# Two-layer pre-norm attention on one core: one more of the eight additions and the residuals given to adding DMA transfers, bias on ScalarE, v stored by channel halves

## The chip, the core and the metric

One core of a Trainium2 chip runs the whole program. The time is device microseconds of one execution, the median of the runs; a profiled execution of the same kernel gives the trace. Engines are named as in the profile: PE is TensorE (PEld its weight loads), DVE VectorE, ACT ScalarE, POOL GpSimd and SP SyncE. POOL and SP issue the DMA transfers; transfers that add into their destination are issued by POOL.

## The reference, cut to what matters

16 images of 256 channels x 32 x 32 go through two layers. Each layer normalises over groups of the last axis, projects q, k and v, and attends over the 1024 positions in 4 heads of 64 channels; the scores have a term of relative positions.

```python
xf = gn(x).reshape(b, 256, 1024)                   # 16 groups, eps 1e-5
q, k, v = (einsum('oc,bcn->bon', W, xf) + bias for W, bias in ...)
sim  = einsum('bhdi,bhdj->bhij', q, k)
qpos = einsum('hdi,bhdj->bhij', rel_h + rel_w, q)
attn = softmax(sim + qpos, axis=-1)
x = x + einsum('bhdn,bhmn->bhdm', v, attn).reshape(x.shape)   # twice, with the second layer's weights
```

Everything is float32. The bias of v can be added after the attention, since each row of `attn` sums to one.

## The kernel before

**Units, stages, blocks.** A unit is one image in one layer; 32 units run in a fixed order in which the second layer of an image comes at least four units after its first. A unit u has four blocks of work, one for each pair of heads `pr` (128 channels: channel half 0 or 1) and each half of 512 query positions. The text calls them b0 (pr 0, half 0), b1 (pr 0, half 1), b2 (pr 1, half 0) and b3 (pr 1, half 1). b0 is written out in `block_with_q` (every unit but the first), b3 in `block_with_values` (every unit but the last), b1 and b2 in `block`; the last unit's b2 and b3 are in `block_without_pieces`. T0 is the moment when TensorE ends b3, T1 when it ends b0, T2 b1 and T3 b2, so b3 runs from T3 to the next T0.

**One block.** For each of eight tiles j of 128 key positions: VectorE writes the term of positions into a PSUM tile (`seed`, L446), TensorE adds the scores (`scores`, L482), ScalarE takes the exponential into a tile p (L491). `add_up` (L521, L523) sums the tiles p on VectorE into `acc`; the last of them, j = 7, is added by a DMA transfer (`add_last`, L554). Then `fold`, `stack_up`, `fold_again` and `fold_stack` bring the partition sums down by further adding transfers (the rows of `stack` halve five times: D, R, R/2, R/4, R/8 with R = 32), `spread_sums` spreads them into `den_all` by four transfers of SP, and `reciprocals` (L633) takes them up on VectorE three to four blocks after the exponentials. TensorE meanwhile forms the products with v (`attend`, L537) in two stretches, and ScalarE copies the result out of PSUM into a tile `od` (`take_out`, L598). About a unit later `normalise` (L648) multiplies that tile by the reciprocals, and `add_residual` (L655) adds it and the bias of v to x, both on VectorE; a layer-1 unit's x is then stored by SP.

**Order.** Nothing is scheduled by a planner: each engine runs its instructions in the order in which the functions below issue them, and so do the queues of POOL and SP, whose transfers wait in line for what the first of them waits for. A transfer that adds to bytes that an earlier transfer writes waits, on POOL, until that one has landed. At the head of VectorE's work in b0, b1 and b2 stand the additions 5 and 6 of the block before; in b3 it is addition 6 alone, since 5 of b2 is made in b2.

**Between blocks.** In b3 the v of the next unit is formed by a scheme of seven products instead of eight (`Values`): its operands are sums of quarters of the normalised x, made by `sum_copies` on SP and `sum_additions` (L335) on POOL during b2. The group statistics of unit u+2 end in b3: rstd (L237) and nshift (L239) are computed on POOL, behind b3's transfers, and ScalarE applies them from b0 on (L248).

**Tiles in rings.** A tile's buffer is taken again when as many tiles of its tag have been allocated as there are buffers, and the first instruction that writes the new tile waits for the last that used the old one. `od` has three, p ten, `acc` three, x five:

```python
outs[u, pr] = opool.tile([P, 2, HALF], F32, tag="od", name=f"od_{u}_{pr}", bufs=3)   # L597, in take_out, half 0
before = blocks[n - 6][:2] if n > 5 else None       # b2: the tile (u-1, 0) is finished in this block
before = blocks[n - 5][:2] if n > 4 else None       # b3: the tile (u-1, 1)
```

In b2, `finish(*before)` comes ahead of that block's `take_out`, in b3 `normalise` and `add_residual` do. The PSUM bank from which b2's `take_out` reads is the one into which b3's first products of v go (`pw`, by the order in `ring`).

Of the kernel before, what the change touches and what calls it, by code (L numbers as in the profile page):

```python
# [9 lines left out]
F32 = mybir.dt.float32  # L10
# [3 lines left out]
ALU = mybir.AluOpType  # L14
# [3 lines left out]
P = 128  # L18
# [25 lines left out]
def flat(ap):  # L44
    return ap.rearrange("p w h -> p (w h)")
# [7 lines left out]
def fast_path(ctx, tc, sh, x, layers, out, W, den_all, good, flag):  # L53
# [26 lines left out]
    nc = tc.nc  # L80
# [119 lines left out]
    def filled(tag, name, value):  # L200
        pm = psum2(tag, name)[:, :, :G]
        nc.vector.memset(pm, value)
        return pm
# [82 lines left out]
    def values(u, g, pv):  # L286
        l = units[u][1]
        if g == 0:
            vts[u] = vpool.tile([P, NT, C], F32, tag="v", name=f"v_{u}")
        pv = pv.rearrange("p a (b c) -> p a b c", c=C)  # L290

        def products(t):
            for i in range(2):
                for cc in range(CC):
                    for rs, a in BANKS[t]:
                        for x, c in enumerate(QUARTERS):
                            j0 = (4 * g + 2 * a + i) * P + x * D
                            yield nc.tensor.matmul(
                                pv[c, a, i, :],
                                xns[u][rs, cc, j0 : j0 + D],  # L300
                                W.wv[l][rs, cc, :],
                                start=(t == 0 and cc == 0 and i == 0),
                                stop=(t == 1 and cc == CC - 1 and i == 1),
                                skip_group_check=True,
                            )

        def out_of_psum():
            nc.scalar.copy(
                vts[u][:, 4 * g : 4 * g + 4, :].rearrange("p (a b) c -> p a b c", a=2), pv
            )  # L310

        return stretches(products), out_of_psum
# [27 lines left out]
    class Values:  # L340

        def __init__(self, u, pw):
            l = units[u][1]
            x, t = quarters_of_x(u), sums_x[u]
            a11, a12, a21, a22 = W.blocks_of_v(l)
            d, s2, s3, s4 = (W.mixed[l][:, i, :] for i in range(4))
            self.pw = pw
            self.terms = {
                1: (0, x[:, 0, :], a11, True),
                2: (1, x[:, 2, :], a12, True),  # L350
                3: (0, x[:, 3, :], s4, False),
                4: (1, t[:, 3, :], a22, False),
                5: (0, t[:, 0, :], d, False),
                6: (0, t[:, 2, :], s2, False),
                7: (1, t[:, 1, :], s3, True),
            }
            vts[u] = vpool.tile([P, NT, C], F32, tag="v", name=f"v_{u}")
            self.v = vts[u]
            self.done = {}

# [35 lines left out]
            )  # L396

        def out(self, oc, nh):
            return self.v[:, nh * 4 : nh * 4 + 4, oc * P : (oc + 1) * P]

        def keep(self, oc, nh, sign):

# [38 lines left out]
    def seed(blk, j, tag):  # L441

        u, pr, half = blk
        ps = psum2(tag, f"ps_{u}_{pr}_{half}_{j}")
        ab = abt[u, pr][:, :, j, :]
        nc.vector.tensor_tensor(  # L446
            ps.rearrange("p h (w y) -> p h w y", y=H),
            ab[:, :, :H].unsqueeze(2).to_broadcast([P, 2, XH, H]),
            ab[:, :, H + half * XH : H + (half + 1) * XH]
            .unsqueeze(3)  # L450
            .to_broadcast([P, 2, XH, H]),
            ALU.add,
        )
        seeds[blk, j] = ps
# [60 lines left out]
    def add_up(blk, j):  # L515
        u, pr, half = blk
        if j == 0:
            return
        if j == 1:
            accs[blk] = apool.tile([P, 2, HALF], F32, tag="acc", name=f"acc_{u}_{pr}_{half}")  # L520
            nc.vector.tensor_tensor(accs[blk], probs[blk, 0], probs[blk, 1], ALU.add)  # L521
        else:
            nc.vector.tensor_tensor(accs[blk], accs[blk], probs[blk, j], ALU.add)  # L523
# [3 lines left out]
    def attend(blk, po):  # L527

        u, pr, half = blk

        def products(t, js=range(NT)):
            for j in js:
                p = probs[blk, j]
                for rs, a in BANKS[t]:
                    for h, c in enumerate(QUARTERS):
                        c0 = pr * P + h * D
                        yield nc.tensor.matmul(  # L537
                            po[c, a, :QUART],
                            vts[u][rs, j, c0 : c0 + D],
                            p[rs, h, a * QUART : (a + 1) * QUART],  # L540
                            start=(t == 0 and j == 0),
                            stop=(t == 1 and j == NT - 1),
                            skip_group_check=True,
                        )

        return stretches(products)
# [3 lines left out]
    R = P // 4  # L550
    stacks = {}

    def add_last(blk):
        nc.gpsimd.dma_start(accs[blk], probs[blk, NT - 1], accum_op=ALU.add)  # L554

    def fold(blk):

# [98 lines left out]
        if l == NL - 1:  # L656
            nc.sync.dma_start(flat(out[b, pr * P : (pr + 1) * P]), xs)

    def add_by_dma(u, pr):
        b, l = units[u]  # L660
        xs = xt[b][:, pr, :]
        nc.scalar.activation(xs, xs, AF.Identity, bias=W.bv[l][:, pr : pr + 1])
        nc.gpsimd.dma_start(xs, outs.pop((u, pr)).rearrange("p a n -> p (a n)"), accum_op=ALU.add)

    def store(u, pr):
        b = units[u][0]
        nc.sync.dma_start(flat(out[b, pr * P : (pr + 1) * P]), xt[b][:, pr, :])

    def finish(u, pr):
        normalise(u, pr)  # L670
        add_residual(u, pr)
# [85 lines left out]
    def block(n):  # L757
# [112 lines left out]
            add_up(blk, 5)  # L870
        if n in (2, 6):
            W.mix(n // 4)
        if before:
            finish(*before)
        if two and half == 1 or n == 0:
            mean_out()
        if stacked:
# [14 lines left out]
    def block_with_q(n):  # L892

        blk = blocks[n]
        u = blk[0]
        r0, r1, r2, r3 = ring
        previous, after, summed = blocks[n - 1], blocks[n + 1], blocks[n - 4][:2]
        folded = n - 1 < FOLDED
        add_up(previous, 5)
        add_up(previous, 6)  # L900
        add_last(previous)
        for j in range(1, 4):
            scores(blk, j)
        first, first_out = project(u, 1, "q", psum2(r3, f"pq_{u}_1"))
        first(0)
        norms(u, 0, 0)
        seed(blk, 4, r1)
        scores(blk, 4)
        norms(u, 0, 1)
        seed(blk, 5, r2)  # L910
        scores(blk, 5)
        add_up(blk, 1)
        fold_stack(*summed, R // 8)
        spread_sums(*summed)
        fold(previous)
        first(1)
        first_out()
        seed(blk, 6, r0)
        scores(blk, 6)
        stack_up(previous)  # L920
        add_up(blk, 2)
        seed(blk, 7, r1)
        scores(blk, 7)
        add_up(blk, 3)
        seed(after, 0, r2)
        add_up(blk, 4)
        if n in check:
            next(checks)
        norms(u, 0, 2)
        po = psum2(r3, f"po_{n}")  # L930
        values_of_p = attend(blk, po)
        values_of_p(0)
        scores(after, 0)
        fold_again(previous)
        ring[:] = r2, r0, r1, r3
        for j in range(1, 4):
            seed(after, j, ring[j % 3])
        reciprocals(*summed)
        norms(u, 0, 3)
        values_of_p(1)  # L940
        take_out(blk, po)
        pos[n] = po

    def block_with_values(n):
# [6 lines left out]
        two = u + 2 < NU  # L951
        v = Values(u + 1, psum2(r3, f"pw_{u + 1}"))

        add_up(previous, 6)
        scores(blk, 1)
        add_up(blk, 1)
        one = v.half(1, HI, False), v.half(1, LO, True)
        two_halves = score_half(blk, 2, 0), score_half(blk, 2, 1)
        v.stage("1", (two_halves[0], two_halves[1]), (one[0], one[1]), 0)
        add_last(previous)  # L960
        scores(blk, 3)
        v.stage("1", (two_halves[0], two_halves[1]), (one[0], one[1]), 1)
        v.keep(0, 0, 1.0)
# [20 lines left out]
        v.keep(1, 1, -1.0)  # L984
        fold_stack(*stacked, R)
        stack_up(previous)
        add_up(blk, 2)
        seed(after, 0, r1)
        v.combine(1, 1, ALU.subtract)
# [2 lines left out]
            next(checks)  # L992
        po = psum2(r2, f"po_{n}")
        values_of_p = attend(blk, po)
        values_of_p(0, range(NT // 2))
        v.pair("4", 3, 4, 0)
        if two:
            mean_out = norm_var(u + 2, filled(r0, f"pm_{n}", EPS / 2))
        values_of_p(0, range(NT // 2, NT))
        scores(after, 0)  # L1000
        v.pair("4", 3, 4, 1)
        v.keep(0, 1, -1.0)
# [12 lines left out]
        fold_stack(*stacked, R // 4)  # L1015
        seed(after, 2, r3)
        if before:
            add_residual(*before)
        seed(after, 3, r1)
        values_of_p(1)  # L1020
        take_out(blk, po)
# [9 lines left out]
    def block_without_pieces(n, half):  # L1031
# [39 lines left out]
        if not last:  # L1071
            after = blocks[n + 1]
            seed(after, 0, f0)
            add_up(blk, 4)
            values_of_p(0)
            scores(after, 0)
            seed(after, 1, f1)
            seed(after, 2, f2)
            reciprocals(*summed)
            normalise(*before)  # L1080
            add_by_dma(*before)
            seed(after, 3, f0)
            values_of_p(1)
            nc.gpsimd.drain()
            take_out(blk, po)
            return
# [450 lines left out]
```

## Time and profile before

| | us |
|---|---|
| median of 3 runs | 2628.89 |
| lowest and highest | 2628.64, 2631.62 |
| the profiled execution | 2630.66 |
| its span, first to last instruction | 2627.2 |
| PE busy | 2542.0 |
| DVE busy | 2340.3 |
| ACT busy | 1953.9 |
| POOL busy | 907.2 |

The span is what the trace covers; the profiled execution's own time is 3.5 us longer, for what lies around it. A busy PE is not a PE at its peak, since matmuls are pipelined and four small ones run beside one another on quarters of the array. Rows of a group give busy us, mean ns of one, and the idle time before with what ended it. A timeline row gives the start, the length and, in brackets, the idle time before. Two DVE instructions of 1.22 us in a row start 1.135 us apart. Of the DMA queues, q0 carries POOL's transfers, q1 SP's.

### The profile page before, as it was taken

What the parts mean: (1) busy time and instruction counts of PE and PEld (TensorE: products, weight loads), DVE (VectorE), ACT (ScalarE), POOL (GpSimd) and SP (SyncE); (2) the same over time, 40 slices, a digit from 0 to 9 for tenths busy, and PEclk for the clock granted to TensorE, in tenths of its full rate; (3) what the DMA queues carried; (4) which work ended last, traced back from release to release, by engine and by line L of the source; (5) the groups of instructions that cost most, each with busy time, mean ns of one, the idle gap of its engine ahead of it and who ended that gap; (6) DMA issues with size and microseconds to landing.
All of it is one profiled execution on the core that took longest, in us unless ns stands there. A gap on an engine that the chain in (4) does not pass through costs nothing.

```text
span 2627.2 us, 94070 instructions
## 1 busy us (share of the span) xinstructions
PE 2542.0 (97%) x41192; PEld 1419.2 (54%) x41192; DVE 2340.3 (89%) x2244; ACT 1953.9 (74%) x3917; POOL 907.2 (35%) x969
## 2 busy tenths in 40 slices
PE   8999999999999999999999999999999999999998
PEld 4555555555555555555555555555555555555554
DVE  7898998889888898998989888888889898898988
ACT  6778777778777787777877778777778777787654
POOL 1333333333333333333333333333333333333330
PEclk9999999999999999999999999999999999999999
DMA  3555545565556555556645565556565555555552
GB/s 92 110 112 114 107 97 107 118 138 116 99 117 136 113 114 103 111 117 126 124 102 112 113 128 114 114 112 116 120 138 115 106 97 117 112 108 101 104 117 75
DMA packets 158064, 295.23 MB, mean 112 GB/s; under 512 B 56392, under 2 KB 57928, under 8 KB 157648
## 3 DMA queue, kind: packets, MB, share of 16 engines
q0 software_dynamic: 75040, 170.74, 39.3%
q1 hardware_dynamic: 82608, 118.41, 15.0%
q8 instruction: 326, 5.34, 0.8%
q14 instruction: 90, 0.74, 0.1%
HBM read 51.78 MB, written 17.30 MB: 26 GB/s over the span
## 4 chain that ended last, share of the span: by engine, by line
PE 75%; DVE 18%; issue 3%; ACT 2%; DMA 1%; SPq 0%; DVEq 0%
PE po L537 27%; PE ps L482 26%; DVE ps L446 9%; PE pk L268 8%; PE pw L367 5%; PE pq L268 4%; DVE acc L523 4%; PE pa L423 2%; DVE acc L521 2%; DVE x L655 1%; DVE v L409 1%; ACT v L403 1%; PE ps L502 1%; ACT p L491 1%; DMA out_dram<-x 1%
## 5 line engine op out<-in xcount | busy, mean ns | idle before, releaser
L491 ACT ACTIVATE p<-ps,shift 128x1024 f32<-128x1024 f32 x993 | 1070.6, 1113 | 473.9 <-PE ps L482 462.2
L446 DVE TENSOR_TENSOR ps<-abt 128x1024 f32<-128x1024 f32 x1018 | 1229.3, 1228 | 144.6 <-ACT p L491 71.9
L482 PE MATMUL ps<-q,k 64*64 64x512 f32 x7944 | 994.8, 593 | 56.0 <-DVE ps L446 51.0
L537 PE MATMUL po<-p,v 64*64 64x256 f32 x16384 | 943.2, 376 | 1.2 <-issue 1.2
L537 PEld LDWEIGHTS po<-p,v 64*64 64x64 f32 x16384 | 653.3, 133 | 302.5 <-issue 61.3
L523 DVE TENSOR_TENSOR acc<-acc,p 128x1024 f32<-128x1024 f32 x643 | 780.7, 1214 | 6.0
L482 PEld LDWEIGHTS ps<-q,k 64*64 64x64 f32 x7944 | 293.4, 133 | 462.6 <-DVE ps L446 227.1
L583 POOL DMA_DIRECT2D stack<-stack x310 | 314.6, 1015 | 236.7 <-DMA stack<-stack 186.7
L578 POOL DMA_DIRECT2D stack<-acc x248 | 213.8, 974 | 345.5 <-DMA stack<-acc 289.9
L559 POOL DMA_DIRECT2D acc<-acc x124 | 104.4, 842 | 447.2 <-DMA acc<-p 439.7
L268 PE MATMUL pk<-xn,Wk 64*64 64x512 f32 x2048 | 242.9, 589 | 0.0
L268 PE MATMUL pq<-xn,Wq 64*64 64x512 f32 x2048 | 242.8, 589 | 0.0
L554 POOL DMA_DIRECT2D acc<-p x124 | 109.5, 883 | 359.9 <-ACT p L491 210.1
L248 ACT ACTIVATE xn<-x,nshift,rstd 128x128 f32<-128x128 f32 x496 | 209.5, 493 | 0.0
L190 ACT ACTIVATE junk<-x,neg 128x128 f32<-128x128 f32 x505 | 197.9, 400 | 0.0
L335 POOL DMA_DIRECT2D t<-xn x93 | 106.3, 1143 | 236.5 <-DMA t<-t 187.7
L598 ACT COPY od<-po 128x512 f32<-128x512 f32 x127 | 74.4, 586 | 137.7 <-PE po L537 137.7
L521 DVE TENSOR_TENSOR acc<-p,p 128x1024 f32<-128x1024 f32 x128 | 156.1, 1219 | 1.4 <-ACT p L491 1.4
L268 PEld LDWEIGHTS pq<-xn,Wq 64*64 64x64 f32 x2048 | 78.3, 133 | 140.9 <-issue 132.2
L268 PEld LDWEIGHTS pk<-xn,Wk 64*64 64x64 f32 x2048 | 75.2, 133 | 123.3 <-issue 123.0
L367 PE MATMUL pw<-mixed,t 64*64 64x128 f32 x2976 | 138.2, 273 | 3.5 <-issue 3.5
L367 PEld LDWEIGHTS pw<-mixed,t 64*64 64x64 f32 x2976 | 116.2, 133 | 45.4 <-DVE v L409 22.7
(95 smaller groups left out, 1915.8 us busy)
## 6 DMA issues: line engine op xcount, KB each, us to landing
acc<-p POOLq DMA_DIRECT2D x124, 512.0 KB, 5.1
rden<-rd SPq DMA_DIRECT2D x126, 256.0 KB, 5.2
acc<-acc POOLq DMA_DIRECT2D x124, 256.0 KB, 3.9
t<-xn POOLq DMA_DIRECT2D x62, 512.0 KB, 5.8
x<-in_x_dram SPq DMA_DIRECT2D x32, 512.0 KB, 4.2
stack<-acc SPq DMA_DIRECT2D x248, 64.0 KB, 2.2
stack<-acc POOLq DMA_DIRECT2D x248, 64.0 KB, 3.1
t<-xn SPq DMA_DIRECT2D x31, 512.0 KB, 3.4
```

The source lines that it names most:

```text
L190: nc.scalar.activation(junk, grouped(xt[units[u][0]], g), func, accum_out=into[:, g : g + 1], **bias)
L248: nc.scalar.activation(grouped(xns[u], g), grouped(xt[units[u][0]], g), AF.Identity, bias=shift[:, g : g + 1], scale=rstd[:, g : g + 1],)
L268: yield nc.tensor.matmul(pk[c, nh, :], w[l][rs, cc, c0 : c0 + D], xns[u][rs, cc, nh * HALF : (nh + 1) * HALF], start=(t == 0 and cc == 0), ...
L367: yield nc.tensor.matmul(self.pw[c, a, part * P : (part + 1) * P], x[rs, j0 : j0 + D], w[rs, :], start=first and not whole and part == 0, ...
L446: nc.vector.tensor_tensor(ps.rearrange("p h (w y) -> p h w y", y=H), ab[:, :, :H].unsqueeze(2).to_broadcast([P, 2, XH, H]), ab[:, :, H + h ...
L482: nc.tensor.matmul(ps[c, h, :], a[hs, j0 : j0 + D], b[hs, columns], start=bool(tag) and i == 0, stop=i == len(terms) - 1, skip_group_check ...
L491: nc.scalar.activation(p, ps, AF.Exp, bias=W.shift)
L521: nc.vector.tensor_tensor(accs[blk], probs[blk, 0], probs[blk, 1], ALU.add)
L523: nc.vector.tensor_tensor(accs[blk], accs[blk], probs[blk, j], ALU.add)
L537: yield nc.tensor.matmul(po[c, a, :QUART], vts[u][rs, j, c0 : c0 + D], p[rs, h, a * QUART : (a + 1) * QUART], start=(t == 0 and j == 0), s ...
L578: nc.gpsimd.dma_start(at, acc[R:D, h, :], accum_op=ALU.add)
L583: nc.gpsimd.dma_start(stack[:rows_], stack[rows_ : 2 * rows_], accum_op=ALU.add)
```

## The change

- `add_last` gets a first tile: in b0 and b3 it adds tiles 6 and 7 of the block before by two transfers, one after the other into the same `acc`, and `add_up(previous, 6)` goes from VectorE. In b3 it moves from behind the first products of v to the head of the block.
- `add_residual` is replaced for units 0 to 29: `normalise` stays, and `add_by_dma` adds the `od` tile to x by a transfer of POOL (512 KB), in b2 for half 0 (behind the last `sum_additions`) and in b3 for half 1 (at its end). The bias is added to x ahead of that, by ScalarE in b3 (`bias_x`, two instructions), a unit before the transfer.
- The stores of layer-1 units move with it: half 0's from b2 to b3 (behind `stack_up`), half 1's from b3 to b0 (ahead of the reciprocals' store).
- v is laid out as [channel half][tile][128] instead of [tile][256], so that a half's four tiles are one run of 512 elements where `keep` and `combine` write; `attend` reads its weights from there.
- In b3 five tiles' products with v, not four, stand ahead of the fourth pair of v's products, and three, not four, behind it.

```diff
-            vts[u] = vpool.tile([P, NT, C], F32, tag="v", name=f"v_{u}")
+            vts[u] = vpool.tile([P, CC, NT, P], F32, tag="v", name=f"v_{u}")
...
         def out(self, oc, nh):
-            return self.v[:, nh * 4 : nh * 4 + 4, oc * P : (oc + 1) * P]
+            return self.v[:, oc, nh * 4 : nh * 4 + 4, :]
...
-                            vts[u][rs, j, c0 : c0 + D],
+                            vts[u][rs, pr, j, h * D : (h + 1) * D],
...
-    def add_last(blk):
-        nc.gpsimd.dma_start(accs[blk], probs[blk, NT - 1], accum_op=ALU.add)
+    def add_last(blk, j0=NT - 1):
+        for j in range(j0, NT):
+            nc.gpsimd.dma_start(accs[blk], probs[blk, j], accum_op=ALU.add)
...
-    def add_by_dma(u, pr):
+    def bias_x(u, pr):
         b, l = units[u]
         xs = xt[b][:, pr, :]
         nc.scalar.activation(xs, xs, AF.Identity, bias=W.bv[l][:, pr : pr + 1])
+
+    def add_by_dma(u, pr):
+        xs = xt[units[u][0]][:, pr, :]
         nc.gpsimd.dma_start(xs, outs.pop((u, pr)).rearrange("p a n -> p (a n)"), accum_op=ALU.add)

     def store(u, pr):
-        b = units[u][0]
-        nc.sync.dma_start(flat(out[b, pr * P : (pr + 1) * P]), xt[b][:, pr, :])
+        b, l = units[u]
+        if l == NL - 1:
+            nc.sync.dma_start(flat(out[b, pr * P : (pr + 1) * P]), xt[b][:, pr, :])
...
# block (b2)
-        if before:
+        if before and last_unit:
             finish(*before)
+        elif before:
+            normalise(*before)
+            add_by_dma(*before)
...
# block_with_q (b0)
+        before = blocks[n - 6][:2] if n > 5 else None
         add_up(previous, 5)
-        add_up(previous, 6)
-        add_last(previous)
+        add_last(previous, NT - 2)
...
+        if before:
+            store(*before)
         reciprocals(*summed)
...
# block_with_values (b3)
-        add_up(previous, 6)
+        add_last(previous, NT - 2)
         scores(blk, 1)
...
-        add_last(previous)
         scores(blk, 3)
...
         stack_up(previous)
+        if before:
+            store(before[0], 0)
...
-        values_of_p(0, range(NT // 2))
+        values_of_p(0, range(5))
         v.pair("4", 3, 4, 0)
         if two:
+            for pr in range(CC):
+                bias_x(u, pr)
             mean_out = norm_var(u + 2, filled(r0, f"pm_{n}", EPS / 2))
-        values_of_p(0, range(NT // 2, NT))
+        values_of_p(0, range(5, NT))
...
         if before:
-            add_residual(*before)
+            add_by_dma(*before)
```

More of the change, by code (lines that the diff above doesn't have):

```diff
@@ L308, in out_of_psum @@
             nc.scalar.copy(
-                vts[u][:, 4 * g : 4 * g + 4, :].rearrange("p (a b) c -> p a b c", a=2), pv
+                vts[u][:, :, 4 * g : 4 * g + 4, :].rearrange("p o n c -> p n o c"),
+                pv.rearrange("p a b (o c) -> p (a b) o c", c=P),
             )
@@ L356, in __init__ @@
             }
-            vts[u] = vpool.tile([P, NT, C], F32, tag="v", name=f"v_{u}")
+            vts[u] = vpool.tile([P, CC, NT, P], F32, tag="v", name=f"v_{u}")
             self.v = vts[u]
@@ L535, in products @@
                     for h, c in enumerate(QUARTERS):
-                        c0 = pr * P + h * D
                         yield nc.tensor.matmul(
                             po[c, a, :QUART],
-                            vts[u][rs, j, c0 : c0 + D],
+                            vts[u][rs, pr, j, h * D : (h + 1) * D],
                             p[rs, h, a * QUART : (a + 1) * QUART],
@@ L1080, in block_without_pieces @@
             normalise(*before)
+            bias_x(*before)
             add_by_dma(*before)
```

## The prediction

> **What bounds the kernel now.** I read the busy row, then the stages of one unit, the chain of waits of b0, and the queues on both sides of T3.
>
> ```profile
> PE 2542.0 (97%) x41192; PEld 1419.2 (54%) x41192; DVE 2340.3 (89%) x2244; ACT 1953.9 (74%) x3917; POOL 907.2 (35%) x969
> ...
> core 0: us, PE busy (x) PEld busy (x) DVE busy (x) ACT busy (x) POOL busy (x), PEclk, DMA share, GB/s
> 1302.70:1325.14 22.44, 21.95 (x517) 16.64 (x512) 19.15 (x21) 12.15 (x14) 7.79 (x9) 1.00 0.57 119
> 1325.14:1344.90 19.76, 18.11 (x228) 8.23 (x224) 18.73 (x18) 15.65 (x33) 7.90 (x8) 1.00 0.33 57
> 1344.90:1363.16 18.26, 18.26 (x300) 9.60 (x296) 16.18 (x17) 16.34 (x36) 6.68 (x8) 1.00 0.52 102
> 1363.16:1383.80 20.64, 20.64 (x260) 9.79 (x256) 18.42 (x17) 17.41 (x43) 6.77 (x7) 1.00 0.75 159
> ```
>
> These are b3, b0, b1, b2: 81.1 us per unit. TensorE fills b1 and b2 to the end; a lighter VectorE is worth nothing there. In b0 it has 1.65 us without work, and 2.55 in all against back-to-back products (scores 0.86 us a tile, projections 1.72, value products 3.45, from the timeline's steps: 8 x 0.86 + 2 x 1.72 + 2 x 3.45 = 17.2). The chain of b0 names the cause:
>
> ```profile
> 1324.46 1.19 DVE x L655
> 1325.64 1.14 DVE ps L446
> 1326.79 1.14 DVE acc L523
> ...
> 1329.09 2.36 DVE ps L446 x2
> ```
>
> The residual (L655) and additions 5 and 6 stand before the seed for which TensorE waits. The change removes two of these three. So its aim is right; its price is on two in-order queues:
>
> ```profile
> 1377.78 1.22 POOL L335 DMA_DIRECT2D t<-xn  x1 [6.40 <-DMA t<-t]
> 1384.04 0.86 POOL L335 DMA_DIRECT2D t<-xn  x1 [2.62 <-DMA t<-xn]
> 1386.51 0.85 POOL L554 DMA_DIRECT2D acc<-p  x1 [1.61 <-DMA stack<-acc]
> 1393.56 0.81 POOL L559 DMA_DIRECT2D acc<-acc  x1 [5.33 <-DMA acc<-p]
> 1403.12 3.23 POOL L237 TENSOR_TENSOR rstd<-var,mhalf 128x16 f32<-128x16 f32 x1
> 1406.43 1.32 POOL L239 TENSOR_TENSOR nshift<-neg,rstd 128x16 f32<-128x16 f32 x1
> ...
> 1383.86 0.59 ACT L598 COPY od<-po 128x512 f32<-128x512 f32 x1 [0.39 <-PE po L537]
> 1401.76 1.11 ACT L491 ACTIVATE p<-ps,shift 128x1024 f32<-128x1024 f32 x1 [5.20 <-PE ps L482]
> ...
> acc<-p POOLq DMA_DIRECT2D x124, 512.0 KB, 5.1
> x<-od POOLq DMA_DIRECT2D x1, 512.0 KB, 6.1
> ```
>
> POOL stands still until a transfer that its next one builds on has landed (1393.56); behind it wait rstd and nshift, which ScalarE needs at T0 + 3.9.
>
> **The change, part by part.**
>
> VectorE: 62 additions go (an addition every 1.135 us in the timeline) and 60 of the 62 residuals (1.19). In b0 seed 4 could then start when exponential 1 ends, T0 + 2.0 instead of T0 + 3.95, and the stage falls from 19.8 to about 17.5 (the 17.2 above plus 0.3 at seed 7). b3 is 22.4 in the mean, 22.1 in its quiet instances; with less on VectorE and the fifth product step (which covers some of the 0.95 us per unit for which weight loads wait on L409) I take 21.6. b2 gains nothing. Gain: 3.1 us per unit.
>
> v by halves: the same counts and sizes. L409 takes 688 ns for 512 elements and L446 1228 for 1024, so 1.05 ns per element beyond 148 ns fixed; the split rows show no toll to win back: 0 (±0.05 each).
>
> ScalarE: 60 biases at 1.14 (L662). Both go into the 5.20 us idle before 1401.76, where ScalarE waits for scores: 0, and up to 2.3 per unit if that cover is gone.
>
> SP: the two stores move behind stack_up. By the times below their data has landed before SP is there; each costs the reciprocals' store behind it 0.34 us of issue, which the 7 us from reciprocal to spread value hide: 0.
>
> POOL, 122 more transfers, about 0.55 us apart when they need not wait: two new waits.
>
> First, the `od` ring. It has three buffers; tile (u-1,0) is number 2u-2 and (u,1) is 2u+1: the same buffer. b2 of unit u ends with take_out writing (u,1). Before, the residual's read of (u-1,0) ended 2.5 us ahead of it. Now a 512 KB transfer reads that buffer, issued behind the last sum_addition, which goes out at T3 - 0.8 to T3 + 1.9 over the units (mean 0.2). So: issue at T3 + 1.0. Ahead of it the 256 KB of t has 1.6 us to move (q0 moved 170.74 MB in 39.3% of 16 engines' span, 3.17 us per 512 KB). Data to T3 + 6.0, landing at about T3 + 6.8; the measured 6.1 alone would give T3 + 7.1. take_out stands at T3 + 0.06 today and runs from 6.9: behind it all exponentials of b3, and TensorE's first value product, which takes the PSUM bank that it frees. b3: 21.6 + 6.9 = 28.5. Bounds 5.5 and 8.
>
> Does the stall halve the clock? The tail shows it:
>
> ```profile
> 2617.00:2620.00 3.00, 0.00 (x0) 0.00 (x0) 1.59 (x3) 0.59 (x1) 0.00 (x0) 1.00 0.03 1
> 2620.00:2623.00 3.00, 0.19 (x2) 0.11 (x2) 0.82 (x5) 0.00 (x0) 0.00 (x0) 0.77 0.22 87
> 2623.00:2627.00 4.00, 0.00 (x0) 0.00 (x0) 0.00 (x0) 0.00 (x0) 0.00 (x0) 0.50 0.06 14
> ```
>
> 0.77 over 2620 to 2623 puts the drop to half at 2621.6, 4.6 us after the last product. The Trainium skill (TensorE: Matmul & The Clock Gate, Part 1) says half speed after an idle window of about 3.4 us and full speed after as long a busy one; nothing in mid-run here shows it. By it each stall costs another 1.7 to 3.4 us of half-speed work; without it 0. I take 2.
>
> TensorE's sum: 28.5 + 2 + 17.5 + 18.3 + 20.6 = 86.9.
>
> Second, POOL's chain. Transfer 6 of b2 goes out at T3 + 1.6, behind t and x: data to 9.1, some more for the 512 KB of rden beside it (1.7 if all in its way), landing near 10.5. Only then can transfer 7 go (11.0), and fold follows at 16.1, where it was at 9.8: +6.3. Everything after it on POOL moves along: nshift ends at 30.3 (24.0 in this unit; over the units 1.2 earlier, so 29.1). T0 is now at 28.5 or later, so ScalarE just escapes. In b0 again: R/4, x of half 1 (+0.9), transfer 6 (+1.8) landing +8.9 (0.9 short of two times 3.17 in its queue), transfer 7, fold_stack R/8 +9.5; den_all 4.55 later than transfer 7 goes (as from 1410.65 now) at +13.4, four issues 3.3, landing 1.9 after the last: +18.7, so T3 + 47.8. VectorE wants it at T1 - 1.1 = 44.9 (46.9 with the slow clock). Behind the waiting reciprocal stand additions 5 and 6 and seed 4 of b1 (3.7 us), for which TensorE waits, then 14.5 of b1 (14.2 from that tile's products to T2 now, and 0.3 at seed 7) and 20.6 of b2: 47.8 + 3.7 + 14.5 + 20.6 = 86.6.
>
> A page prices this otherwise: the Trainium skill (DMA: Bandwidth & Descriptors, Anatomy of one DMA) has 2.0 us + bytes / 436 GB/s, so 3.2 for 512 KB. x would land at T3 + 4.2, the stall be 4.2, POOL's chain never last: 21.6 + 4.2 + 17.5 + 18.3 + 20.6 = 82.2, some 2664 us. The trace has 5.1 and 6.1 for these adding transfers; I use the trace.
>
> What else is held longer: p tiles 6 and 7 of b3 are read until T3 + 43 and overwritten (ten buffers) by b1's first exponentials, the later at T1 + 0.9, 46.9 or after: free, with 4 us to spare; if that cover is gone, ScalarE waits at the head of b1 as long as the transfer is late.
>
> Sum: 87.0 a unit, +5.9, in 30 units: +177. The profiled execution took 2630.7 (span 2627.2), 1.8 above the median of 2628.9; so 2808, or 2806 on the median.
>
> **The rivals.** A change under 0.2% (5 us) can't be told from none here.
> 1. *Both waits* (0.62): 2806; with contention 90 us a unit, 2900.
> 2. *Only the ring's wait, POOL's chain covered* (0.30, with or without clock): transfer 6 lands 5 us after issue, as acc<-p does at the median, and nshift moves by 3. Unit 84.9 without the slow clock: +3.8 x 30, 2743. With a stall of 5.5: 83.5, 2700. For it: 55% DMA share before, some 70% after. Against: acc<-p took 7.1 us at 1386.51 with less beside it.
> 3. *Faster: x lands before take_out wants the buffer* (0.06). One mechanism: POOL gets past sum_additions so early, or moves so fast, that the ring's wait is below the 3.1 us won. It decides at a landing at T3 + 3.1; fully hidden, 3.1 x 30: 2536. For it: the transfer's sources are ready at 1380.0. Against: it is queued behind 1384.04.
> 4. *Nothing moves* (0.02): the wait equals the gain, 2629.
>
> That the products or v's layout alone do the work is excluded by the 0 above.
>
> **How the numbers follow.** Forecast 2806, rival 1. The range runs from rival 2's lower end (2700, with a little for less wait: 2690) to rival 1's upper (2900); outside remain 3, 4 and some of the tails. Faster 0.06, same 0.02, slower 0.92.
>
> **What would show it.** L598 on ACT waits for DMA x<-od, 30 times, about 6.5 us each; a PE gap of 6 to 7 us at each start of b3, granted clock below 1.00 there; on POOL a wait of acc<-p for DMA acc<-p, 62 times, 5 to 9 us; DVE r waits for DMA den_all; b0 near 17.5 where nothing waits; DVE busy down by about 142 us, ACT up by 68. Wrong, if take_out at T3 still waits for PE alone, or if b3 stays below 23 us.

## The result, and the profile after

| | before | after |
|---|---|---|
| median, us | 2630.26 | 2933.22 |
| lowest to highest, 4 runs each | 2628.64 to 2633.51 | 2918.34 to 2941.18 |
| the profiled execution | 2630.66 | 2918.34 |
| its span | 2627.2 | 2914.5 |

The ratio is 1.1144 (95%: 1.1096 to 1.1191). The change is slower by about 300 us; forecast were 177 more, and the upper end of the range, 2900, lies below what was measured.

The busy row first, then the stages b3, b0, b1, b2 of one unit. The columns of the second view are those shown with the prediction: length, busy time of PE, PEld, DVE, ACT, POOL, granted clock, DMA share, GB/s.

```profile
PE 2604.5 (89%) x41192; PEld 1495.0 (51%) x41192; DVE 2198.0 (75%) x2122; ACT 2011.4 (69%) x3977; POOL 1045.7 (36%) x1091
...
1443.62:1476.17 32.55, 23.58 (x516) 17.82 (x512) 17.09 (x18) 14.12 (x16) 14.79 (x15) 0.84 0.61 118
1476.17:1494.12 17.95, 17.50 (x229) 8.90 (x224) 15.42 (x14) 15.53 (x33) 4.56 (x6) 1.00 0.58 106
1494.12:1514.10 19.98, 18.89 (x300) 9.32 (x296) 17.09 (x18) 16.36 (x36) 7.16 (x10) 1.00 0.51 100
1514.10:1534.74 20.64, 20.64 (x260) 9.79 (x256) 18.20 (x17) 17.40 (x43) 8.85 (x11) 1.00 0.80 162
```

VectorE has lost the 142 us that were to go, and the core is slower all the same: TensorE fell from 97 to 89% of a longer span. b0 is the stage that the change shortened (19.76 to 17.95 here); b3 grew by ten, at a clock of 0.84; b1 grew by 1.7; b2 is what it was. In the mean over the units:

| us | b3 | b0 | b1 | b2 | unit |
|---|---|---|---|---|---|
| before | 22.4 | 19.8 | 18.3 | 20.6 | 81.1 |
| predicted | 28.5 + 2 clock | 17.5 | the rest, waiting | 20.6 | 87.0 |
| after | 32.4 | 17.9 | 19.7 | 20.6 | 90.6 |

Thirty units of 9.5 us more are 285 of the 288 us by which the two profiled executions differ. The table of waits names both places (engine, line, what it waited for: us in all, times, longest):

```profile
ACT od L599 <- DMA x<-od: 272.4, 30, 11.5
PE pw L368 <- ACT od L599: 247.7, 30, 10.7
POOL acc L555 <- issue: 219.8, 28, 10.2
POOL acc L555 <- DMA acc<-p: 127.7, 20, 9.3
POOL acc L555 <- ACT p L492: 103.4, 55, 6.4
DVE r L634 <- DMA den_all<-stack: 65.1, 30, 3.6
```

The first two are the ring: ScalarE's `take_out` waits 9.1 us a unit for the transfer that adds `od` to x, and TensorE waits behind it for the PSUM bank. The next three are POOL, held at the transfers 6 and 7, the second above all; "issue" means that the profile shows no releaser, and its timeline below shows where it stands. In b0 the profile puts the second's wait down to an exponential; but as in b3 it goes out just behind the landing of the first, 0.5 us later in the mean. The last is VectorE at the head of b1, 2.2 us a unit. The timelines of POOL, ScalarE and VectorE of that unit (start, length, in brackets the idle time before), with T3 = 1443.62:

```profile
1444.54 1.21 POOL L336 DMA_DIRECT2D t<-xn  x1
1445.10 1.52 POOL L667 DMA_DIRECT2D x<-od  x1
1445.64 1.86 POOL L555 DMA_DIRECT2D acc<-p  x1
1455.78 0.85 POOL L555 DMA_DIRECT2D acc<-p  x1 [8.28 <-issue]
...
1460.74 0.81 POOL L560 DMA_DIRECT2D acc<-acc  x1 [3.24 <-DMA acc<-p]
1470.55 3.97 POOL L237 TENSOR_TENSOR rstd<-var,mhalf 128x16 f32<-128x16 f32 x1 [1.07 <-DVE var L235]
1474.60 0.97 POOL L239 TENSOR_TENSOR nshift<-neg,rstd 128x16 f32<-128x16 f32 x1
...
1452.89 0.59 ACT L599 COPY od<-po 128x512 f32<-128x512 f32 x1 [9.59 <-DMA x<-od]
1467.14 2.19 ACT L663 ACTIVATE x<-x,bv 128x1024 f32<-128x1024 f32 x2
...
1495.66 0.25 DVE L634 RECIPROCAL r<-den_all 128x16 f32<-128x16 f32 x1 [2.55 <-DMA den_all<-stack]
```

The x transfer stands behind the last `sum_additions`, 1.5 us after T3; ScalarE, ready at T3, copies 9.3 us after it. `rstd` comes not behind POOL alone here: it also waits 1.07 us for VectorE's variance, which is late itself. The two biases of x (1467.14) show no wait in front and none behind.

### The profile page after: what moved, and what is told of

It reads as the page before. It is cut to its first block, busy times and chain, and to the rows that moved or that the text cites. A ratio compares the mean times of both kernels' runs of the same rounds, so it can differ in the third digit from the quotient of the medians.

```text
span 2914.5 us, 94154 instructions
## 1 busy us (share of the span) xinstructions
PE 2604.5 (89%) x41192; PEld 1495.0 (51%) x41192; DVE 2198.0 (75%) x2122; ACT 2011.4 (69%) x3977; POOL 1045.7 (36%) x1091
## 4 chain that ended last, share of the span: by engine, by line
PE 43%; DMA 35%; DVE 9%; issue 4%; ACT 3%; SPq 3%; POOL 2%; DVEq 0%; ACTq 0%; POOLq 0%
PE po L537 15%; PE ps L483 14%; DMA t<-xn 9%; PE pw L368 8%; DMA x<-od 8%; DMA acc<-p 5%; DVE ps L447 5%; DMA stack<-stack 4%; DMA stack<-acc 4%; SPq L592 3%; DVE acc L524 2%; PE pq L268 2%; ACT p L492 2%; DMA t<-t 2%; DMA acc<-acc 2%
## 5 line engine op out<-in xcount | busy, mean ns | idle before, releaser
L483 PE MATMUL ps<-q,k 64*64 64x512 f32 x7944 | 1028.8, 607 | 44.6 <-DVE ps L447 39.9
L537 PE MATMUL po<-p,v 64*64 64x256 f32 x16384 | 941.6, 377 | 0.0
L537 PEld LDWEIGHTS po<-p,v 64*64 64x64 f32 x16384 | 647.7, 133 | 306.2 <-issue 44.3
L524 DVE TENSOR_TENSOR acc<-acc,p 128x1024 f32<-128x1024 f32 x581 | 706.6, 1216 | 5.0
L483 PEld LDWEIGHTS ps<-q,k 64*64 64x64 f32 x7944 | 318.5, 135 | 437.7 <-issue 223.2
L584 POOL DMA_DIRECT2D stack<-stack x310 | 303.9, 980 | 302.7 <-DMA stack<-stack 194.8
L368 PE MATMUL pw<-Wv,xn 64*64 64x128 f32 x1984 | 176.5, 331 | 247.9 <-ACT od L599 247.7
L555 POOL DMA_DIRECT2D acc<-p x186 | 200.3, 1077 | 502.3 <-issue 219.8
L368 PEld LDWEIGHTS pw<-Wv,xn 64*64 64x64 f32 x1984 | 143.1, 166 | 283.0 <-ACT od L599 255.0
L268 PEld LDWEIGHTS pq<-xn,Wq 64*64 64x64 f32 x2048 | 85.7, 134 | 134.7 <-issue 134.1
L237 POOL TENSOR_TENSOR rstd<-var,mhalf 128x16 f32<-128x16 f32 x31 | 123.5, 3982 | 47.9 <-DVE var L235 47.8
```

Source lines behind the costliest of these rows:

```text
L268: yield nc.tensor.matmul(pk[c, nh, :], w[l][rs, cc, c0 : c0 + D], xns[u][rs, cc, nh * HALF : (nh + 1) * HALF], start=(t == 0 and cc == 0), ...
L368: yield nc.tensor.matmul(self.pw[c, a, part * P : (part + 1) * P], x[rs, j0 : j0 + D], w[rs, :], start=first and not whole and part == 0, ...
L483: nc.tensor.matmul(ps[c, h, :], a[hs, j0 : j0 + D], b[hs, columns], start=bool(tag) and i == 0, stop=i == len(terms) - 1, skip_group_check ...
L537: yield nc.tensor.matmul(po[c, a, :QUART], vts[u][rs, pr, j, h * D : (h + 1) * D], p[rs, h, a * QUART : (a + 1) * QUART], start=(t == 0 an ...
L555: nc.gpsimd.dma_start(accs[blk], probs[blk, j], accum_op=ALU.add)
L584: nc.gpsimd.dma_start(stack[:rows_], stack[rows_ : 2 * rows_], accum_op=ALU.add)
```

## The experiments

Before's medians beside them were 2632.85 (e1 to e4), 2632.0 (e7 to e10) and 2633.69 (e5, e11 to e13).

**One wait without the other.** The first of three kernels gives `od` a fourth buffer, paid for by one of the two of `rden`; the second gives residuals and stores back to VectorE and SP's old places and keeps the sixth additions as transfers; the third gives only the sixth additions back.

```diff
-  ... tag="od", ... bufs=3)          # e1: after, with
+  ... tag="od", ... bufs=4)          #     rden in one buffer, the last unit's in a tile of the x ring
```

> The changed kernel with four od buffers instead of three (the room comes from one rden buffer instead of two, whose uses never overlap; the last unit's two rden tiles take a buffer of the x ring). take_out of b2 no longer writes the buffer that the transfer of half 0 reads. Theory RING (the 9 us wait of take_out at T3 and the half-speed clock that follows it are the loss, and POOL's longer chain lies beneath them): L599 waits for PE alone, b3 falls from 32.4 to about 22, clock back to 1.00, unit 79, total about 2560. Theory CHAIN (POOL's queue from T3 to the reciprocals of b0, 51.5 us in the changed kernel, sets the unit whatever TensorE does in between): the ring's wait goes but ScalarE then waits 4 to 5 us for nshift in b0 and VectorE 5 us or more for den_all; unit about 89, total 2850 to 2890.

```diff
-            normalise(*before)        # e2: after, with
-            add_by_dma(*before)
+            finish(*before)           #     b3 likewise; bias_x taken out, stores where they were
```

> The changed kernel with the residuals (and their stores) put back on VectorE as before; the sixth additions of two blocks stay transfers, v's layout and the five products stay. RING: no transfer reads od, so no wait at T3; b0 about 18.7, b3 22, total about 2585. CHAIN: transfer 7 still waits on POOL for transfer 6 twice a unit; without the x transfers ahead of it each lands about 3 us sooner, so the way from T3 to the reciprocals is about 44 us: nshift late by 1.7 us for ScalarE, reciprocals late by 3 us or more, unit 83, total about 2690.

```diff
-        add_last(previous, NT - 2)    # e3: after, with
+        add_up(previous, 6)
+        add_last(previous)            #     b3's behind v.keep, where it was
```

> The changed kernel with the two sixth additions put back on VectorE; the residuals stay transfers with three od buffers. RING: the wait at T3 stays, about 1 us shorter since no acc transfer is beside it; b3 about 31, total 2860 to 2900. CHAIN: POOL's queue is shorter by two landings (12 us), so only the wait at T3 is left: b0 18 to 19, b1 18.3, b3 30 to 31, unit 88, total about 2830. The two differ little here; b1 is the tell: 18.3 in both if the reciprocals no longer wait for den_all.

| | median | ratio, 95% | b3 | b0 | b1 | unit |
|---|---|---|---|---|---|---|
| e1_od4 | 2909.21 | 1.1024 to 1.1062 | 24.0 | 21.9 | 24.0 | 90.5 |
| e2_no_x | 2690.61 | 1.0200 to 1.0234 | 22.3 | 19.4 | 21.3 | 83.6 |
| e3_no_six | 2881.18 | 1.0919 to 1.0962 | 31.9 | 18.6 | 18.3 | 89.4 |

Waits of e1, of e2 and of e3:

```profile
DVE r L635 <- DMA den_all<-stack: 160.9, 31, 8.0
ACT xn L248 <- POOL nshift L239: 99.6, 27, 5.8
```

```profile
DVE r L634 <- DMA den_all<-stack: 102.7, 32, 5.4
ACT xn L248 <- POOL nshift L239: 38.6, 17, 7.5
```

```profile
ACT od L599 <- DMA x<-od: 263.1, 30, 10.8
```

In e1 the wait for x is gone from `take_out`, and the unit keeps its length to 0.1 us: what b3 no longer loses is lost in b0, where ScalarE now waits for nshift, and in b1, where the reciprocals wait 5.2 us instead of 2.2. In e3 the ring alone costs 8.3 us a unit (89.4 against 81.1). So the two waits lie over one another: each alone is worth eight to nine and a half, both 9.5. That is how the prediction set them, as the later of two sums and not as their total. e2 shows that the chain is long with both kinds of transfer on POOL, 9.4 in e1; with the sixth additions alone it is 2.5.

**Both taken away.** e4_od4_no_six is e1's and e3's edit together.

> Four od buffers and the two sixth additions on VectorE, so that of the change only the residuals' transfers, the bias on ScalarE, the layout and the five products are left, without the ring's wait. RING: about 2560, like four buffers alone (b0 1 us longer by the addition). CHAIN: this one alone of the four is faster than the kernel before: b0 18.7, b3 22, unit 79.5, total about 2580; and it is about 300 us faster than four buffers alone.

2641.32 (ratio 1.0024 to 1.0049, 15 runs): the 290 us are gone, so nothing large beside the two waits is at work, and e1's single `rden` buffer, which this kernel has too, is not what kept e1 slow. But the gain of 3 us a unit does not come. b0 is 18.6 and b1 18.5, b3 23.9. There TensorE stops between small products of v:

```profile
PE pw L368 <- issue: 32.7, 26, 2.5
PE ps L483 <- issue: 12.5, 4, 3.3
```

With the few at L537 these waits come to 46.7 us, where e5 below has 8.2. Twenty of the pauses last 1.2 to 3.3 us, and at sixteen of these a 16 KB transfer of the queue that the profile calls "instruction" starts within 1 us of the pause's beginning. Before has shorter ones (0.3 to 1 us). That instructions arrive late beside busier transfers would fit; it was not tried, and `rden` with one buffer is another difference of this kernel. So some 39 of the 60 us that are missing against the expected 2580 lie in these pauses; their cause, and the rest, stay open.

**What sets the landing of x.** `take_out` started 8.7 us after T3 where 6.9 were worked out. Three kernels on top of e3 take one suspect each: e8_x_first issues the transfer ahead of the last `sum_additions`; e9_last_on_dve takes away the 512 KB that follow it on its queue, by adding b2's tile 7 on VectorE; e11_rden_late lets ScalarE issue the two `rden` transfers (512 KB in all) behind `take_out`, not SP at the same time as x.

```diff
+            sum_additions(u + 1, 2)      # e8: in b2, behind add_by_dma instead of ahead of it
-        add_last(previous)               # e9: in b3
+        add_up(previous, 7)
-        (SP) rden[...] <- rd             # e11: in b2
+        (ACT) rden[...] <- rd            #      in b3, behind take_out
```

> Additions 6 on VectorE as in the kernel without them as transfers (2881 us, where the wait at T3 stood alone: x landed 8.4 us after T3), three od buffers, and one move: in b2 POOL issues the transfer of half 0 ahead of the last sum_additions instead of behind it, so about 4 us earlier and with only its successor beside it. If the time of landing sets the loss, take_out waits until T3 + 2 to 3, the clock stays at 1.00, b3 is 24 to 25 and the total 2650 to 2680. If something else holds take_out, b3 stays near 32.

> As the kernel with additions 6 on VectorE (2881 us), and in b3 tile 7 of b2 too is added on VectorE, so that no acc transfer goes out behind x at T3. If transfers of one queue are served one after the other (my prediction's assumption), x lands at T3 + 8.4 as before and the total stays within 15 us of 2881 (one addition more on VectorE). If transfers in flight share the engines, x lands near T3 + 6.3, b3 falls by 2 to 3 us and the total to about 2800.

> As the kernel with additions 6 on VectorE (2881 us, x landing 8.4 us after T3), but the two rden transfers of 256 KB that SP starts 3 us after T3 are issued by ScalarE behind take_out, so after x has landed (normalise wants them 8 us later still). If they share the engines with x and make up what my sum missed (1.6 us between the landing that I worked out, T3 + 6.8, and the measured one), x lands near T3 + 7, b3 falls by 1.5 us and the total to about 2835. If x takes its time without them, take_out's wait and the total stay (2870 to 2890).

| | median | ratio, 95% | wait of take_out for x, a unit | b3 |
|---|---|---|---|---|
| e3_no_six | 2881.18 | 1.0919 to 1.0962 | 8.8 | 31.9 |
| e8_x_first | 2798.08 | 1.0600 to 1.0650 | 5.4 | 29.2 |
| e9_last_on_dve | 2894.00 | 1.0969 to 1.1013 | 8.9 | 32.3 |
| e11_rden_late | 2854.30 | 1.0818 to 1.0851 | 7.1 | 31.1 |

The waits of e8 and of e11:

```profile
ACT od L599 <- DMA x<-od: 161.0, 30, 9.3
```

```profile
ACT od L599 <- DMA x<-od: 213.2, 30, 8.7
```

and the transfers of e3 and of e11 (KB each, median us from issue to landing):

```profile
x<-od POOLq DMA_DIRECT2D x61, 512.0 KB, 6.3
```

```profile
x<-od POOLq DMA_DIRECT2D x61, 512.0 KB, 5.6
rden<-rd ACTq DMA_DIRECT2D x60, 256.0 KB, 4.6
```

In e8 the time follows the landing: `take_out` starts at T3 + 5.0 where it was at 8.4 in e3, b3 is 2.7 us shorter, the run 83 us. The hoped-for rest did not come, since the x transfer still goes out only 1.1 us ahead of T3 in the mean (0.9 behind it in e3); `fold_again`, which waits in front of it, holds POOL. e9 shows that a transfer behind x on the same queue does not delay it (266.7 us in 30 waits against 263.1). e11 shows what does: transfers of SP's queue at the same time. Without them `take_out` starts at T3 + 6.7, 1.7 us earlier than in e3 and where the prediction had it (6.9). b3 is shorter by 0.8 only, which is the 27 us. The other 0.9 is the price of the edit itself: the two issues take ScalarE 1.2 us of each unit, ahead of an exponential, which starts 7.2 us after `take_out` where it did so after 6.0 in e3. In one unit, and in all:

```profile
1420.84 1.12 ACTq L644 DMA_DIRECT2D rden<-rd  x2
1422.01 1.11 ACT L513 ACTIVATE p<-ps,shift 128x1024 f32<-128x1024 f32 x1 [0.71 <-issue]
...
ACT p L513 <- issue: 22.5, 29, 2.0
```

**The clock by itself.** e10_busy is e3 with fourteen more products of 128x128x256 at the end of b2, into a part of the PSUM bank that nobody reads, so that TensorE is not idle while it waits.

> As the kernel with additions 6 on VectorE (2881 us), and TensorE is kept busy in the wait at T3: 14 products of 128 x 128 x 256 into the unused half of the value products' PSUM bank at the end of b2, some 6 us of work that nobody reads. take_out still waits for x at T3 + 8.4. If the half-speed clock after the stall costs what the profile's half-speed stretches suggest (3.4 to 6.8 us of work at half speed a unit, so 1.7 to 3.4 us), the granted clock is back at 1.00, b3 falls by about 2 us and the total to about 2815. If the clock costs nothing that shows, the total is 2881 or a little more.

2838.66 (1.0770 to 1.0817), 42.5 us below e3, or 1.4 a unit; 0.3 of this is that `take_out` starts a little sooner. One b3 of e3 and one of e10:

```profile
1421.31:1452.04 30.73, 24.11 (x516) 18.42 (x512) 17.92 (x19) 14.21 (x16) 13.09 (x13) 0.89 0.55 107
```

```profile
1394.59:1423.09 28.50, 28.32 (x545) 21.91 (x548) 17.92 (x19) 14.11 (x16) 13.12 (x13) 1.00 0.57 114
```

The granted clock of the run rises from 0.959 to 0.993, and half-speed stretches fall from 31 to 8. More work on TensorE is faster; the wait itself remains (`take_out` at T3 + 8.1 for 8.4).

**The chain by itself.** e12_r8_first is e2 with b0's two acc transfers moved behind `fold_stack` R/8 and `spread_sums`.

```diff
         add_up(previous, 5)
-        add_last(previous, NT - 2)
...
         fold_stack(*summed, R // 8)
         spread_sums(*summed)
+        add_last(previous, NT - 2)
```

> The kernel with the residuals on VectorE and the sixth additions as transfers (2691 us), where in b0 POOL issues fold_stack R/8 (and SP spread_sums) ahead of the two acc transfers instead of behind them; nothing else. If POOL's standing still for transfer 6 is what makes the reciprocals late (102.7 us of VectorE's waits there), those waits go, b1 falls from 21.3 to about 18.5, and the total to 2600 to 2625, with what is left being ScalarE's wait for nshift in b0. If the reciprocals wait for another reason, the total stays near 2690.

2781.09 (1.0526 to 1.0600): 90 us slower than e2, where a gain was expected. Its waits:

```profile
DVE r L634 <- DMA den_all<-stack: 14.5, 7, 7.4
ACT xn L248 <- POOL nshift L239: 149.5, 28, 7.5
```

The reciprocals no longer wait, as meant, and b1 is 18.35. But R/8 now waits for the landing of R/4 with nothing between them, so the acc transfers and all behind them go later: the last `sum_additions` 4.3 us after T3, nshift 9.1 us after T0, and b0 is 23.8. POOL's queue is a round through the whole unit; moving a wait in it did not shorten it.

**What the rest is worth, and a version that is faster.** e5_layout is before with the layout of v and five products ahead of the last step, nothing else.

> The kernel before with two parts of the change alone: v by channel halves and five products ahead of the fourth pair of v's products. The layout at 0 (same counts and sizes) and the products at 0 to -0.9 us a unit: 2605 to 2635, most likely -10 us against before. A layout that costs on weight loads or on ScalarE's strided writes would show as more than +5 us.

2621.10 (0.9938 to 0.9965), 12.6 us less; b3 falls from 22.4 to 22.2. e7_half1 keeps of the change only what meets no wait: half 0's residual stays on VectorE, the sixth additions too (b0's behind seed 5); half 1's residual is a transfer, but issued in b0 behind R/8, `spread_sums` and `add_last`. e13_half1_seed7 also puts b0's own addition 2 behind seed 7.

```diff
+        add_up(previous, 6)              # e7: e5, in b0 behind scores 5
         fold_stack(*summed, R // 8)
         spread_sums(*summed)
+        add_last(previous)
+        add_by_dma(*before)              #     half 1 alone; its bias on ScalarE in b3
         add_up(blk, 1)
...
-        add_up(blk, 2)                   # e13: e7, and
         seed(blk, 7, r1)
         scores(blk, 7)
+        add_up(blk, 2)
```

> A version made from what the others showed: half 0's residual stays on VectorE in b2 (which TensorE fills anyway, and where its transfer would meet the od ring), half 1's residual is a transfer with its bias on ScalarE, issued in b0 behind fold_stack R/8, spread_sums and add_last; all additions 6 on VectorE, b0's behind seed 5 instead of at the head; layout and five products as changed. No wait at T3, POOL's way to den_all not longer than before. b0 17.9 to 18.2, b1 18.3, b2 20.6, b3 22: 79 a unit, total about 2565; if the added transfer delays b3's instruction supply or den_all as well, 2600 to 2640.

> The version with half 1's residual as a transfer (2605 us), where b0 loses 1.18 us at seed 7, which stands on VectorE behind additions 6, 1 and 2; here addition 2 goes behind seed 7. b0 from 19.0 to 17.9, 31 times: total about 2571. If the next limit of b0 is as near as 0.3 us, 2595.

e7: 2605.46 (0.9879 to 0.9914); TensorE stands 1.2 us ahead of score 7 of b0, since three additions are in front of seed 7. e13: 2585.28 (0.9800 to 0.9830), b0 18.1, b1 18.8, b3 22.1: 1.8% less than before, 12% less than the change. Its busy row, and all that is left of waits for x:

```profile
PE 2532.0 (98%) x41192; PEld 1447.9 (56%) x41192; DVE 2304.7 (89%) x2214; ACT 1979.4 (77%) x3947; POOL 942.1 (36%) x999
...
ACT junk L190 <- DMA x<-od: 25.6, 6, 5.3
```

VectorE is as busy as before; 98% of TensorE comes from what stands ahead of a seed. The x transfer is met by ScalarE's statistics six times in the run, where in after every unit's `take_out` met it.

## Why the prediction was wrong

**Right: direction, mechanisms and places.** `take_out` waits for x 30 times, the clock falls in b3, POOL stands between transfers 6 and 7, the reciprocals wait, b0 is 17.9 (17.5), DVE falls by 142, ACT rises by 57 (68). The biases, the stores and the p tiles cost nothing visible. The failure is one of size. POOL's chain, the later of the two sums, was put at 86.6 us a unit and measured 90.6; TensorE's was put at 86.9 and measured 89.2. The step that failed is the price of the transfers behind T3, first of all x, which was given the whole rate (6.9 us, measured 8.7), and in POOL's chain also a stretch that was to keep its length and grew by 1.5. The later sum sets the time, and the range, which ended at 90 us a unit, ended just below it.

**TensorE's sum, 86.9 predicted.** Without the wait of b1 for the reciprocals it measured 32.4 + 17.9 + 18.3 + 20.6 = 89.2. The terms:

| term | predicted | measured | from |
|---|---|---|---|
| b3 without a stall | 21.6 | 22.2 | e5 |
| take_out starts at T3 + | 6.9 | 8.7 | after |
| clock | 2 | 1.4 | e10, and e3: 31.9 - 22.2 - 8.3 |
| b0 | 17.5 | 17.9 | after |

+0.6, +1.8, -0.6 and +0.4 make 2.2 of the 2.3. The term that failed is the second: the prediction counted the 512 KB of `rden` only against transfer 6 ("some more for the 512 KB of rden beside it"), and let x, ahead of it in the same queue, have the whole rate. e11 prices that at 1.7 us. The change itself moved `rden` there. With no residual in front of them, VectorE takes up the reciprocals of b2 1.3 us earlier, at T3 - 0.5 instead of T3 + 0.9 in the mean, and `rden`, which is made from them, goes out at T3 + 1.8 instead of 3.8, next to x (the way between them is 0.7 shorter as well); in e2, with the residuals back, it is 4.2. In the units shown (T3 = 1383.80 before, 1443.62 after):

```profile
1384.62 0.24 DVE L633 RECIPROCAL r<-den_all 128x16 f32<-128x16 f32 x1
1388.66 1.90 SPq L640 DMA_DIRECT2D rden<-rd  x2
...
1443.13 0.24 DVE L634 RECIPROCAL r<-den_all 128x16 f32<-128x16 f32 x1
1445.40 1.12 SPq L641 DMA_DIRECT2D rden<-rd  x2
```

**POOL's chain, 47.8 + 38.8 = 86.6 predicted.** Measured, it is 51.5 from T3 to the reciprocals and 39.1 from there to the next T3: 90.6, the unit. Along the chain, from T3, in the mean:

| | predicted | measured |
|---|---|---|
| x issued | 1.0 | 1.2 |
| transfer 6 | 1.6 | 1.8 |
| transfer 7 | 11.0 | 11.9 |
| fold | 16.1 | 17.4 |
| nshift ends | 29.1 | 31.9 |
| reciprocals | 47.8 | 51.5 |

Transfer 7 goes out 0.9 late; that `rden` is the cause here too was not tried. The largest step that was missed, 1.5 us, lies between fold and nshift: the prediction let that stretch keep its length "along" POOL, but rstd needs the variance, which comes out of VectorE behind a TensorE that stands still and then runs at half speed. It is ready at T3 + 26.7 in the mean (16.3 before), and rstd starts 0.2 us later. The waits, 28.2 us of them in one at the start of the run:

```profile
POOL rstd L237 <- DVE var L235: 47.8, 21, 28.2
```

So in this kernel the one wait fed the other, where the prediction had them side by side. That this made the unit longer is not shown: in e1, without the stall, the variance is ready at T3 + 18.0, yet the transfers 6 and 7 land later (fold at 18.5), nshift ends at 31.3 and the unit is 90.5. Another 0.9 lies in b0; its cause stays open.

**The clock.** Measured are 1.4 us a stall. The estimate from the page (Trainium skill, TensorE: Matmul & The Clock Gate, Part 1) was 1.7 to 3.4, and without it 0: the measurement is nearer to the page than to nothing. Every b3 with the stall has a half-speed stretch of 6.8 or 10.2 us, multiples of 3.41, beginning 3 to 6 us after T3, which fits the page's windows of about 3.4 us. Why the price is below the estimate was not tried.

**The page's price of a transfer.** The 3.2 us estimated for 512 KB by the page's formula (Trainium skill, DMA: Bandwidth & Descriptors, Anatomy of one DMA), which the prediction weighed and left, are far from what was seen: the medians are 6.6 for x and 5.4 for acc. The trace was the better guide, and still too low for a transfer beside others.

**The rivals.** Both waits was the case, at its contended end: 90 a unit were named there, and its 2900 was to be the upper end. The ring alone was given 2743 and is 2881 (e3); its 84.9 lacked 0.6 in b3, 1.5 of the landing (8.4 in e3), the clock's 1.4, and 1.1 in b0, where e3 has the sixth addition on VectorE again. Rival 3 is excluded by e8 too: even with x issued first, `take_out` starts at T3 + 5.0, not at 3.1. That products and layout do the work by themselves was rightly excluded; they are worth 12.6 us (e5), 8 of it 0.26 a unit in b3, a third of the 0.8 (22.4 to 21.6) that the prediction gave to b3 for them and the lighter VectorE.

## What to carry to other kernels

When an engine's read of a buffer becomes a transfer, ask who writes that buffer next and when: the reader was done 2.5 us early, the transfer 9 us late, and a fourth buffer would have served only with POOL's round shortened too. An in-order queue that carries chained transfers is to be added up as a closed round, with every other engine that must hand it something; relieving one of its waits moves the wait. Price a transfer with all that moves at that moment on any queue, and at the moments that hold after the change: an engine that is relieved hands on its results, and starts their transfers, sooner. Take engine work off the path by order first: the best version here left VectorE nearly as busy as before.

## What the hardware showed beyond what was expected

- Transfers of two queues slow each other: 512 KB on SP's queue held up an adding transfer on POOL's by 1.7 us (e3 to e11), while 512 KB behind it on the same queue did not (wait 263.1 us in e3, 266.7 in e9).
- Issuing two transfers from ScalarE took 1.2 us of it a unit, ahead of its next exponential, and cost b3 0.9 us (e11).
- Products that nobody reads made a kernel 42.5 us faster (e10), most of it by keeping the granted clock at 0.993 instead of 0.959; about a fifth came of an earlier landing.
- TensorE pauses of 1.2 to 3.3 us, most of them inside rows of small products, come together with 16 KB transfers on the instruction queue (e4). Whether these are the cause is open.
